# Fixed slots and a written TensorE order for the heads of a gated cross-attention block

## The chip, the core and the metric

The kernel runs on one core of a Trainium2 chip. The metric is the time of one execution in device microseconds (us). The engines are TensorE (PE; its weight loads are shown as PEld), VectorE (DVE), ScalarE (ACT), GpSimd (POOL) and SyncE (SP), which issues most DMAs.

## What is computed

The block has two gated halves over x of 8 batches x 256 tokens x 512 channels. First comes a cross-attention with 16 heads of 32 channels to a context of 256 rows per batch, in which the query and output projections are quantised to 8-bit integers. Then comes a feed-forward network (FFN) of 1408 hidden channels whose operands are quantised to fp8 after a reordering of columns.

```python
def xattn(x, cond, mask, wq, bq, wk, bk, wv, bv, wo, bo):   # 16 heads
    q = w8a8_linear(x, wq, bq); k = cond @ wk.T + bk; v = cond @ wv.T + bv
    ...
    scores = einsum('bhnd,bhld->bhnl', q, k) * inv_sqrt_d + mask[:, None]
    o = einsum('bhnl,bhld->bhnd', softmax(scores), v)
    return w8a8_linear(o, wo, bo)

def ffn(x, w_gate, w_up, w_down, up_idx, down_idx):
    qx, sx, sc = reorder_quantize_x(x, up_idx)               # fp8 grid
    t = silu(qlinear(qx, w_gate)) * qlinear(qx, w_up)
    return qlinear(reorder_quantize_x(t, down_idx), w_down)

x = x + tanh(g_xattn[0]) * xattn(layernorm(x), ctx, mask, ...)
x = x + tanh(g_ffn[0]) * ffn(layernorm(x), ...)
```

## The kernel before, in words

The program is one unrolled stream. A scheduler places the instructions of each engine by priority and by its own estimate of when operands are ready; that order is then fixed, and each engine executes its list in order, waiting on semaphores. `tc.keep_in_program_order` pins an instruction behind the one that was written before it on its engine. In the FFN all engines are pinned so (`InOrder`, seen as line L61). In the heads only the matmuls of one group of four heads, after the group's first, were pinned to each other (`in_turn`, with high priority).

**Start.** x, the context and the weights are loaded. The key and value weights are transposed in fp32; the query and output weights are quantised and transposed in bf16 (`prep_int8`, tiles `tb_wq`, `tb_wo`). Batch 0 gets its keys, queries and values.

**Heads.** The main loop runs over 8 batches x 8 slots (`NP` = 8, `B` = 8) and two more. Slot `g` is batch `b`, step `i`. The heads come in groups of four. Every second slot does the scores of a group (`scores`, L623, tile `s`): matmuls of 32 rows, four heads beside each other, into PSUM tiles of two banks (`ps_h`, two of them). DVE adds the mask, negates and finds the row's minimum (L638, `sn`, `nm`), ACT takes the exp (L648, `pr`). One slot later two heads are transposed (`transposed`, L664, tile `t`, copied to `pT` by ACT, L673), another slot later a group is multiplied with the values (`weighted`, L682, `poT`, copied to `oT`), and another slot later it is transposed back and normalised (`normalised`, L701 `po`, L705 `rsum`, L707 `o`).

Beside the heads each batch carries these steps:

- `project_kv` of the next batch: two context transposes (L501 `ct`, L504 `cT`), four key pieces (L511 `pk`, L518 `kT`), two value pieces (L527 `pv`, L534 `v`).
- `project_q` of the next batch: quantised rows (L552 `xq`, L560 `qx`), their transposes (L566 `qt`, L571 `qxT`) with a row broadcast of the scales (L356 `rb_sx`), then four query pieces (L577 `pq`, scaled on DVE L584, biased on POOL L587, `qT`).
- `project_out` of the batch before: rows (L225 `mxo`, L319, L320), transposes (L741 `ot`), two products (L752 `py`, L760 `y`), added to x on POOL (L763, L764).
- `quantise_x2` of the batch before: for each of two tiles, statistics and the fp8 grid (L775, L780 `xm`, L225 `mx`, L203, L207, L208), a transpose (`tb_x`), and a store to DRAM (L794).
- `pieces`: the FFN's weights, gathered by row through POOL's DMA queue (L425), masked on POOL (L431), quantised, transposed (`tb_gate`, `tb_up`, `tb_d`), stored and gathered again by column (L444, L477). There are 33 pieces over seven batches.

All of these except the scores use one pool of four PSUM banks (`bank`, tag `m`).

`spread` set the places: the steps of a list were appended to slots `first` to `end` at equal distances, with `kv_steps` from 0 to 6, `q_steps` from 3 to 7 (4 to 7 in batch 0), output and x2 from 3 to 8, pieces over the whole batch. In each slot the four head parts (lags 0 to 3) were written first and the slot's steps behind them:

```python
            for lag in range(4):
                if 0 <= g - lag < B * NP:
                    parts[(g - lag) // NP][lag]((g - lag) % NP)
            for f in slots[i]:
                f()
```

**FFN.** After the heads 16 token tiles pass through gate, up, silu, quantisation and down (L61). The last batch's output projection and x2 run beside its first tiles (`behind_heads`).

Of the kernel before, what the change touches and what calls it, by code (L numbers as in the profile page):

```python
# [29 lines left out]
F32 = mybir.dt.float32  # L30
# [20 lines left out]
class InOrder:  # L51


    def __init__(self, tc, engine):
        self.tc, self.engine = tc, engine

    def __getattr__(self, name):
        method = getattr(self.engine, name)

        def issue(*args, **kwargs):  # L60
            return self.tc.keep_in_program_order(method(*args, **kwargs))  # L61

        return issue
# [3 lines left out]
def tile_flamingo_block(  # L67
# [175 lines left out]
    with ExitStack() as actx:  # L243
# [4 lines left out]

        mv1 = wp.tile([P, NT, 2], F32, tag="mv1", name="mv1")
# [55 lines left out]
        def prep_fp32(n, rows):  # L305
            for k in range(KC):
                wr = rows[k]
                pt = bank(f"pt_{n}{k}")
                for cc in range(KC):
                    nc.tensor.transpose(  # L310
                        pt[:, cc * P : (cc + 1) * P], wr[:, cc * P : (cc + 1) * P], ident
                    )
# [9 lines left out]
        def transpose_bf16(src, dst, n, name):  # L322

            pt = bank(f"tb_{name}", BF16)
            for k in range(n):
                nc.tensor.transpose(
# [22 lines left out]
        def row_bcast(dst, cols, name):  # L349

            n = cols.shape[-1]
            for k0 in range(0, n, 4):
                m = min(4, n - k0)
                pb = bank(f"rb_{name}{k0}")
                for k in range(m):
                    nc.tensor.matmul(  # L356
# [9 lines left out]
        def held_up():  # L366
# [8 lines left out]
            for k in range(KC):  # L375
                oh = tl.tile([P, C], BF16, tag="q8", name=f"oh_{k}", bufs=4)
                nc.vector.tensor_scalar(oh, iota, u_f[:, k : k + 1], None, ALU.is_equal)
                nc.tensor.matmul(
# [13 lines left out]
        def held_down():  # L392
# [4 lines left out]
            for s0, n in ICH:  # L397
                pc = bank(f"count_d{s0}")
                nc.tensor.matmul(
# [93 lines left out]
        def project_kv(b, cr):  # L493
            cT = ld.tile([P, KC, L], F32, tag="cT", name=f"cT_{b}", bufs=1)
            kT = kv.tile([P, KC, L], F32, tag="kT", name=f"kT_{b}")
            v = []

            def transposed(lt):
                pt = bank(f"ct_{b}_{lt}")
                for cc in range(KC):  # L500
                    nc.tensor.transpose(  # L501
# [3 lines left out]
                    cT[:, :, lt * P : (lt + 1) * P], pt.rearrange("p (c o) -> p c o", o=P)  # L505
                )

            def keys(oc):
                pk = bank(f"pk_{b}_{oc}")
                for cc in range(KC):  # L510
                    nc.tensor.matmul(  # L511
                        pk[:, :L],
                        wTf["k"][:, cc, oc * P : (oc + 1) * P],
                        cT[:, cc, :],
# [7 lines left out]
            def values(lt):  # L522
# [3 lines left out]
                for cc in range(KC):  # L526
                    nc.tensor.matmul(  # L527
                        pv,
                        cT[:, cc, lt * P : (lt + 1) * P],
# [11 lines left out]
        def project_q(b):  # L541
            qT = kv.tile([P, KC, S], F32, tag="qT", name=f"qT_{b}")
            qxT = tl.tile([P, KC, S], BF16, tag="qxT", name=f"qxT_{b}")
            sxb = ld.tile([P, S], F32, tag="sxb", name=f"sxb_{b}", bufs=1)

            qx = {}
# [15 lines left out]
            def turned():  # L562
                pt = bank(f"qt_{b}", BF16)
                for nt in range(TPB):
                    for cc in range(KC):
                        nc.tensor.transpose(  # L566
# [3 lines left out]
                        )  # L570
                nc.any.tensor_copy(qxT, pt.rearrange("p (c n) -> p c n", n=S))  # L571
                row_bcast(sxb, sx[:, b * TPB : (b + 1) * TPB], f"sx{b}")

            def queries(oc):
                pq = bank(f"pq_{b}_{oc}")
                for cc in range(KC):
                    nc.tensor.matmul(  # L577
                        pq[:, :S],
                        wT8["q"][:, cc, oc * P : (oc + 1) * P],
                        qxT[:, cc, :],  # L580
# [4 lines left out]
                    qT[:, oc, :], pq[:, :S], s8["q"][:, oc : oc + 1], sxb, ALU.mult, ALU.mult  # L585
# [7 lines left out]
        def attention(b, qT, kT, v, mk):  # L593
# [9 lines left out]
            def in_turn(products):  # L603

                products[0]()
                with tc.high_priority():
                    for product in products[1:]:
                        tc.keep_in_program_order(product())

            def scores(i):  # L610
# [10 lines left out]
                def product(nt, h):  # L621
                    r0 = (h % HPC) * D
                    return nc.tensor.matmul(  # L623
# [7 lines left out]
                in_turn([partial(product, nt, h) for nt in range(TPB) for h in heads])  # L631
# [26 lines left out]
            def transposed(i):  # L658
                for h in (2 * i, 2 * i + 1):
                    pr = probs.pop(h)  # L660
                    pst = bank(f"t_{b}_{h}").rearrange("p (c n) -> p c n", n=S)
                    for nt in range(TPB):
                        for lc in range(LC):
                            nc.tensor.transpose(  # L664
# [11 lines left out]
            def weighted(oc):  # L676
# [3 lines left out]
                def product(lc, h):  # L680
                    r0 = (h % HPC) * D
                    return nc.tensor.matmul(  # L682
# [7 lines left out]
                in_turn([partial(product, lc, h) for lc in range(LC) for h in heads])  # L690
# [6 lines left out]
            def normalised(oc):  # L697
                oT = poT.pop(oc)
                po = bank(f"po_{b}_{oc}")
                for nt in range(TPB):  # L700
                    nc.tensor.transpose(  # L701
# [22 lines left out]
        def project_out(b, o):  # L724
            so = sm.tile([P, TPB], F32, tag="so", name=f"so_{b}")
            qoT = tl.tile([P, KC, S], BF16, tag="qxT", name=f"qoT_{b}")
# [10 lines left out]
            def turned():  # L737
                pt = bank(f"ot_{b}", BF16)
                for nt in range(TPB):
                    for cc in range(KC):  # L740
                        nc.tensor.transpose(  # L741
# [4 lines left out]
                nc.any.tensor_copy(qoT, pt.rearrange("p (c n) -> p c n", n=S))  # L746

            def product(nt):
                t = b * TPB + nt
                py = bank(f"py_{t}")  # L750
                for cc in range(KC):
                    nc.tensor.matmul(  # L752
                        py,
                        qoT[:, cc, nt * P : (nt + 1) * P],
# [13 lines left out]
        def quantise_x2(b):  # L768

            xT = tl.tile([P, KC, S], BF16, tag="x2T", name=f"x2T_{b}", bufs=1)  # L770

            def rows(nt):
                t = b * TPB + nt
# [115 lines left out]
        for g in range(B * NP + 2):  # L889
# [27 lines left out]
            for f in slots[i]:  # L917
                f()
# [212 lines left out]
```

## Time and profile before

| | us |
|---|---|
| median of 4 runs | 678.62 (674.23 to 678.92) |
| the profiled execution | 678.77 |
| its span, first to last instruction | 676.8 |
| mean granted TensorE clock | 0.887 |

Busy shares of the span on the page:

| PE | PEld | DVE | ACT | POOL |
|---|---|---|---|---|
| 525.4 us (78%) | 341.0 (50%) | 523.0 (77%) | 430.1 (64%) | 252.2 (37%) |

The shares are averages over stages with different limits, so a stage has to be read from its own windows. The matmuls are pipelined and their ends are modelled, so a PE that is busy is not a PE at its peak. The first scores start at 42.9 us, the scores of batches 1 to 7 at 102.1, 156.9, 212.0, 265.5, 319.3, 371.1 and 427.1 us, and the first matmul of the FFN at 495.1 us.

### The profile page before, as it was taken

What the parts mean: (1) busy time and instruction counts of PE and PEld (TensorE: products, weight loads), DVE (VectorE), ACT (ScalarE), POOL (GpSimd) and SP (SyncE); (2) the same over time, 40 slices, a digit from 0 to 9 for tenths busy, and PEclk for the clock granted to TensorE, in tenths of its full rate; (3) what the DMA queues carried; (4) which work ended last, traced back from release to release, by engine and by line L of the source; (5) the groups of instructions that cost most, each with busy time, mean ns of one, the idle gap of its engine ahead of it and who ended that gap; (6) DMA issues with size and microseconds to landing.
All of it is one profiled execution on the core that took longest, in us unless ns stands there. A gap on an engine that the chain in (4) does not pass through costs nothing.

```text
span 676.8 us, 10393 instructions
## 1 busy us (share of the span) xinstructions
PE 525.4 (78%) x3591; PEld 341.0 (50%) x3591; DVE 523.0 (77%) x1389; ACT 430.1 (64%) x995; POOL 252.2 (37%) x216
## 2 busy tenths in 40 slices
PE   2697786886994996996899696869387876999962
PEld 1465555654762663674575464447244543555531
DVE  1885696778759679779848899839759998899971
ACT  1467887737856874984894797555635666566661
POOL 4346054432441332433222004440034753477651
PEclk9798798895996997799599796979697998999996
DMA  8930013001250201300142213320000100011000
GB/s 219 356 80 11 24 48 94 17 15 47 64 171 26 85 1 32 94 17 16 32 170 77 74 56 94 109 78 1 7 11 23 50 22 31 32 40 41 31 32 31
DMA packets 27946, 41.64 MB, mean 62 GB/s; under 512 B 7563, under 2 KB 15115, under 8 KB 27894
## 3 DMA queue, kind: packets, MB, share of 16 engines
q1 hardware_dynamic: 19974, 28.25, 12.6%
q0 software_dynamic: 4336, 12.20, 6.2%
q10 hardware_dynamic: 3584, 0.54, 0.6%
q8 instruction: 28, 0.46, 0.3%
q14 instruction: 24, 0.20, 0.1%
HBM read 30.33 MB, written 10.65 MB: 61 GB/s over the span
## 4 chain that ended last, share of the span: by engine, by line
DVE 33%; PE 32%; ACT 17%; issue 9%; POOL 3%; DMA 2%; another core or an unknown queue 1%; ACTq 1%; POOLq 0%; DVEq 0%
PE pk L511 6%; PE t L664 6%; ACT pr L648 5%; DVE sn L638 3%; PE s L623 3%; PE poT L682 3%; DVE mxt L61 3%; PE pv L527 3%; ACT pT L673 3%; DVE s_gate L61 2%; PE p_gate L61 2%; DVE s_up L61 2%; PE p_up L61 2%; DVE xm L780 2%; ACT v_t L61 2%
## 5 line engine op out<-in xcount | busy, mean ns | idle before, releaser
L648 ACT ACTIVATE pr<-sn,nm 128x256 f32<-128x256 f32 x256 | 127.7, 503 | 46.9 <-DVE nm L638 46.7
L638 DVE CUSTOM_DVE_ANT_0 sn<-s,mk 128x256 f32<-128x256 f32 x256 | 97.9, 418 | 19.3 <-ACT pr L648 7.3
L664 PE MATMUL t<-ident,pr 128*128 128x128 f32 x512 | 81.3, 302 | 24.5 <-DVE v L534 12.0
L61 POOL TENSOR_TENSOR tt<-s_up,sl 128x704 f32<-128x704 f32 x32 | 64.9, 2029 | 81.1 <-ACT sl L61 58.4
L623 PE MATMUL s<-kT,qT 32*128 32x256 f32 x512 | 63.2, 492 | 33.1 <-DVE nm L638 23.5
L664 PEld LDWEIGHTS t<-ident,pr 128*128 128x128 f32 x512 | 63.7, 156 | 41.5 <-DVE v L534 13.6
L61 PEld LDWEIGHTS <-xg 128*128 128x128 bf16 x512 | 51.4, 101 | 54.0 <-issue 12.7
L673 ACT COPY pT<-t 128x512 f32<-128x512 f32 x120 | 65.6, 585 | 19.8 <-PE t L664 15.1
L511 PE MATMUL pk<-cT,wkT 128*128 128x256 f32 x256 | 69.4, 426 | 10.1 <-ACT cT L504 6.2
L511 PEld LDWEIGHTS pk<-cT,wkT 128*128 128x128 f32 x256 | 52.6, 213 | 25.1 <-ACT cT L504 6.4
L61 PE MATMUL p_gate<-gateT,xg 128*128 128x352 bf16 x256 | 46.1, 325 | 21.0 <-DVE s_gate L61 21.0
L623 PEld LDWEIGHTS s<-kT,qT 32*128 32x128 f32 x512 | 35.3, 223 | 49.4 <-issue 31.4
L763 POOL TENSOR_TENSOR x_sb<-x_sb,bo_b 128x512 f32<-128x512 f32 x16 | 22.6, 1426 | 96.9 <-ACT xq L552 96.9
L527 PE MATMUL pv<-wvT,cT 128*128 128x512 f32 x128 | 58.3, 599 | 0.1
L648 ACT ACTIVATION_READ_ACCUMULATOR pr<-sn,nm 128x1 f32 x256 | 49.3, 193 | 0.0
L587 POOL TENSOR_SCALAR qT<-qT,bq_c 128x256 f32<-128x256 f32 x32 | 17.9, 567 | 83.6 <-DVE qT L584 62.1
L61 PE MATMUL p_up<-upT,xg 128*128 128x352 bf16 x256 | 46.5, 328 | 0.0
L61 PE MATMUL yp<-wdT,qtT 128*128 128x512 bf16 x176 | 42.4, 391 | 1.9 <-ACT qtT L61 1.9
L61 ACT COPY qtT<-ptq 128x1024 bf16<-128x1024 bf16 (+1 forms) x32 | 22.3, 748 | 32.0 <-PE ptq L61 32.0
L61 ACT ACTIVATE v_t<-tt,rs_t 128x1408 f32<-128x1408 f32 x16 | 23.5, 1470 | 27.9 <-DVE rs_t L61 27.9
L682 PE MATMUL poT<-pT,v 128*32 128x256 f32 x512 | 39.2, 430 | 1.1 <-ACT cT L504 0.7
L527 PEld LDWEIGHTS pv<-wvT,cT 128*128 128x128 f32 x128 | 23.3, 191 | 26.6 <-issue 24.6
(192 smaller groups left out, 1105.7 us busy)
## 6 DMA issues: line engine op xcount, KB each, us to landing
cr<-in_ctx_dram SPq DMA_DIRECT2D x8, 512.0 KB
x_sb<-in_x_dram SPq DMA_DIRECT2D x8, 512.0 KB
out_dram<-yo SPq DMA_DIRECT2D x16, 256.0 KB
wd<-in_L_ffn_w_down_dram SPq DMA_DIRECT2D x4, 704.0 KB
mk<-in_mask_BxSxS_ff_dram SPq DMA_DIRECT2D x8, 256.0 KB
scr_x<-x2T SPq DMA_DIRECT2D x8, 256.0 KB
scr_gate<-gateT SPq DMA_DIRECT2D x1, 1408.0 KB
scr_up<-upT SPq DMA_DIRECT2D x1, 1408.0 KB
```

The lines of the kernel that those rows point to most:

```text
L61: return self.tc.keep_in_program_order(method(*args, **kwargs))
L511: nc.tensor.matmul(pk[:, :L], wTf["k"][:, cc, oc * P : (oc + 1) * P], cT[:, cc, :], start=(cc == 0), stop=(cc == KC - 1),)
L527: nc.tensor.matmul(pv, cT[:, cc, lt * P : (lt + 1) * P], wTf["v"][:, cc, :], start=(cc == 0), stop=(cc == KC - 1),)
L587: nc.gpsimd.tensor_scalar(qT[:, oc, :], qT[:, oc, :], bq_c[:, oc : oc + 1], ISD, ALU.add, ALU.mult)
L623: return nc.tensor.matmul(pss[h][:, nt, :], qT[r0 : r0 + D, oc, nt * P : (nt + 1) * P], kT[r0 : r0 + D, oc, :], start=True, stop=True,)
L638: nc.vector.tensor_tensor_reduce(out=sn[:, nt, :], in0=pss[h][:, nt, :], in1=mk[:, nt, :], scale=-1.0, scalar=3.0e38, op0=ALU.add, op1=ALU ...
L648: nc.scalar.activation(pr[:, nt, :], sn[:, nt, :], AF.Exp, bias=nm[:, nt : nt + 1], scale=-1.0, accum_out=sums[:, nt, h : h + 1],)
L664: nc.tensor.transpose(pst[:, lc, nt * P : (nt + 1) * P], pr[:, nt, lc * P : (lc + 1) * P], ident,)
L673: nc.scalar.copy(pT, pst)
L682: return nc.tensor.matmul(poT[oc][r0 : r0 + D, :], v[0][:, lc, h * D : (h + 1) * D], probsT[h][:, lc, :], start=(lc == 0), stop=(lc == LC ...
L763: nc.gpsimd.tensor_tensor(x_sb[:, t, :], x_sb[:, t, :], bo_b, ALU.add)
L780: nc.vector.scalar_tensor_tensor(xm, x_sb[:, t, :], mv[:, 0:1], mu_b, ALU.subtract, ALU.mult)
```

## The change

Four things are edited together.

1. `in_turn` goes, and all TensorE instructions of the attention stage are issued through `ten`, an `InOrder` whose `kept` is switched on at the first slot. From there TensorE follows the written order. The other engines are still placed by the scheduler.
2. `spread` goes. An `agenda` over all 66 slots takes the steps at slot numbers counted from the batch's start, which may reach into the next batch: the last two key pieces, the second value piece and the last three query pieces of the next batch now stand in that batch's own slots 0 to 3, and the last step of x2 one slot later than the batch's end.
3. Within a slot the steps are no longer all behind the four head parts: a third of them stands behind each of the first three (scores, transposes, products); a single step stands behind the third.
4. Some tiles (`cT`, `qxT`, `sxb`, `qoT`, `x2T`) are allocated at their first use and not when the steps are listed.

```diff
-    def __init__(self, tc, engine):
-        self.tc, self.engine = tc, engine
+    def __init__(self, tc, engine, kept=True):
+        self.tc, self.engine, self.kept = tc, engine, kept
...
-            return self.tc.keep_in_program_order(method(*args, **kwargs))
+            i = method(*args, **kwargs)
+            return self.tc.keep_in_program_order(i) if self.kept else i
...
+        ten = InOrder(tc, nc.tensor, kept=False)
...
-            def in_turn(products):
-
-                products[0]()
-                with tc.high_priority():
-                    for product in products[1:]:
-                        tc.keep_in_program_order(product())
...
-                in_turn([partial(product, nt, h) for nt in range(TPB) for h in heads])
+                for nt in range(TPB):
+                    for h in heads:
+                        product(nt, h)
...
-        def spread(slots, steps, first, end):
-
-            for k, f in enumerate(steps):
-                slots[first + k * (end - first) // len(steps)].append(f)
+        agenda = [[] for _ in range(B * NP + 2)]
+
+        def due(b, steps, slots):
+
+            for f, i in zip(steps, slots, strict=True):
+                agenda[b * NP + i].append(f)
+
+        def evenly(n, first, end):
+            return [first + k * (end - first) // n for k in range(n)]
+
+        KV_AT = (4, 4, 5, 6, 8, 10, 7, 9)
+        Q_AT = (4, 5, 7, 8, 10, 11)
+
+        OUT_AT = (3, 4, 4, 5, 6, 7, 8, 8)
+        PIECES_AT = (0, 1, 2, 4, 5)
...
-                    spread(slots, kv_steps, 0, 6)
-                    spread(slots, q_steps, 4 if b == 0 else 3, 7)
+                    due(b, kv_steps, KV_AT)
+                    due(b, q_steps, Q_AT)
...
-                    spread(slots, project_out(b - 1, o_last) + quantise_x2(b - 1), 3, NP)
+                    due(b, project_out(b - 1, o_last) + quantise_x2(b - 1), OUT_AT)
...
-                    spread(slots, pieces[n0:n1], 4 if b == 0 else 0, NP)
+                    due(b, pieces[n0:n1], evenly(n1 - n0, 4, NP) if b == 0 else PIECES_AT[: n1 - n0])
...
+            ten.kept = True
+
+            n = len(agenda[g])
             for lag in range(4):
                 if 0 <= g - lag < B * NP:
                     parts[(g - lag) // NP][lag]((g - lag) % NP)
-            for f in slots[i]:
-                f()
+                for f in agenda[g][n * lag // 3 : n * (lag + 1) // 3]:
+                    f()
```

## Prediction

> **What bounds the kernel now.** I read the busy time by stage first, cut where the first scores matmul (L623) of each batch starts. The columns are the length, then the busy time of PE, PE's weight loads, DVE, ACT and POOL (instructions in brackets), the granted TensorE clock and the DMA load.
>
> ```profile
> core 0: us, PE busy (x) PEld busy (x) DVE busy (x) ACT busy (x) POOL busy (x), PEclk, DMA share, GB/s
> 51.70:102.10 50.40, 40.26 (x269) 27.49 (x268) 35.92 (x117) 41.19 (x102) 20.27 (x21) 0.90 0.10 28
> 102.10:156.90 54.80, 41.55 (x294) 28.39 (x294) 41.02 (x124) 33.43 (x92) 21.46 (x19) 0.92 0.13 39
> 156.90:212.00 55.10, 46.00 (x325) 30.43 (x325) 39.97 (x135) 37.42 (x105) 18.75 (x18) 0.84 0.27 87
> 212.00:265.50 53.50, 44.53 (x322) 29.58 (x322) 42.38 (x137) 38.83 (x108) 16.95 (x16) 0.88 0.13 40
> 265.50:319.30 53.80, 46.47 (x328) 30.90 (x329) 45.47 (x144) 39.70 (x110) 19.26 (x18) 0.85 0.15 45
> 319.30:371.10 51.80, 47.45 (x323) 31.36 (x323) 37.78 (x132) 39.92 (x115) 11.03 (x12) 0.84 0.27 91
> 371.10:427.10 56.00, 42.86 (x303) 28.40 (x302) 51.02 (x149) 42.66 (x113) 9.93 (x10) 0.85 0.22 68
> 427.10:495.10 68.00, 45.80 (x389) 31.79 (x388) 46.92 (x153) 37.78 (x109) 16.40 (x18) 0.82 0.17 51
> 495.10:676.80 181.70, 139.62 (x894) 80.48 (x890) 150.47 (x194) 98.07 (x106) 96.35 (x58) 0.93 0.09 31
> ```
>
> A batch takes about 54 us (the rows are batches 0 to 7 and the FFN), and no engine is full: in batches 1 to 6 PE is busy for 76 to 92%, DVE for 73 to 91%, ACT for 61 to 77%. The next view cuts batch 4 and its neighbours where the character of the work changes.
>
> ```profile
> 258.00:280.80 22.80, 15.61 (x103) 9.43 (x100) 19.62 (x75) 16.37 (x47) 6.13 (x7) 0.63 0.14 40
> 280.80:312.00 31.20, 31.20 (x237) 21.81 (x239) 26.05 (x70) 23.39 (x62) 13.13 (x12) 1.00 0.15 48
> 312.00:335.40 23.40, 16.05 (x102) 9.77 (x94) 20.20 (x74) 17.07 (x48) 4.32 (x5) 0.64 0.08 23
> ```
>
> So a batch is two stages. For 31 us PE is never idle, at full clock. For 23 us DVE is 86% busy (19.62 of 22.80), PE has little to do, and its clock falls to 0.63. The work is not too much; it is bunched. The order of TensorE's instructions shows why: all projections of the next batch stand between its scores 1 and 3, and after scores 3 come only scores, transposes and the quantising of x2. The waits from 257 to 281 us agree:
>
> ```profile
> ACT v_x L203 <- DVE rs_x L214: 5.2, 1, 5.2
> ACT pr L648 <- DVE nm L638: 3.9, 1, 3.9
> PE s L623 <- DVE mx L212: 3.2, 1, 3.2
> PE t L664 <- DVE v L534: 1.4, 1, 1.4
> ```
>
> The chain of waits for the same stretch alternates between the quantising of x2 and the softmax:
>
> ```profile
> 262.34 0.89 DVE xm L780
> 263.25 0.69 DVE mx L225
> 264.32 4.04 ACT pr L648 x16
> ```
>
> **The change, part by part.** *No arithmetic is added or removed.* Matmuls, copies and DMAs are the same; only their places move. In the built programs the FFN's TensorE order is the same in both, so its 181.7 us stays.
>
> *The start.* With TensorE's order pinned, the first scores stand behind the values and all four transposes of wo. Before, they started at 42.9 us, but scores 1 only at 51.7 us, with one wo transpose left. I start the heads at 52.0 us, and the first group's softmax, which lay beside the values, now comes after: 2.8 us of DVE (eight at 0.344), so 3 us.
>
> *Even slots.* In the built program each pair of slots (four heads) now has TensorE work of about the same kind. From full-clock paces, the distance from one start to the next in an unbroken run (a keys piece 8 x 0.216 = 1.73 us, a values piece 8 x 0.429 = 3.43, two heads' transposes 1.04, 16 scores matmuls 1.08, 16 of poT 1.0, half of py 0.9, pq 0.5, small transposes and row broadcasts 0.3 to 0.6) the four pairs of a steady batch sum to about 11.3, 7.8, 11.6 and 10.7 us: 41 us. Before, the 31.2 us dense stretch plus about 8 us of full-clock work in the sparse one (its instructions at the same paces) give the same 39. DVE's pairs, from its paces (a head's softmax 2 x 0.344, x2 rows 3.6 a tile, a weight piece about 2.2) are 9.3, 10.2, 14.3 and 8, or 42. ACT has about 39. So no engine needs over 42 to 46 us of the 54.
>
> *The limit after.* The most loaded engine becomes DVE. How full can it be? Where it led, it was 86% busy (258 and 312 us, above); in the dense stretch 83% (26.05 of 31.20). I take 0.85 for all, with 0.80 and 0.92 as ends. Batches 1 to 6 hold 41.02+39.97+42.38+45.47+37.78+51.02 = 257.6 us of DVE. At 0.85 that is 303 us against 325 (102.1 to 427.1); at 0.92, 280; at 0.80, 322.
>
> *Batch 0.* Half of the next batch's projections leaves it for batch 1, and ACT is its fullest engine (41.19). Less two kT copies, 40 at about 0.89: 45 us, and the 3 of the start make 48, against 50.4.
>
> *Batch 7.* It took 68 us, with PE and DVE under 70%. It now receives the rest of its own projections (two pk, one pv, three pq). Its pairs sum to PE 15, 8, 6, and DVE about 10 each, so 35 us to its last scores. From there quantising x2 ended the stage: py at 472.2, its transpose at 488.2, the first p_gate at 495.1, 23 us. The second py now stands before the last scores, so I take 18.
>
> *POOL's and SP's queues.* The gather of w_down (L477) now has all eleven issues ahead of qT of batch 7; before, seven were ahead of the second. The store landed about 6.3 us after issue (428.3 to 434.6) and the gathers took 14.8 (434.6 to 449.4). That is 21 us from the middle of pair 3 of batch 6, and batch 7's scores come 18 later: 3 us of stall, with 0 and 10 as ends, all of TensorE behind it. Similarly qT of scores 1 stands behind one or two weight gathers (L425, whose landing POOL waited for by up to 4.4 us); its slack is a slot of 6 us, so I price it at 0, at most 2 us a batch. SP's stores of x2T move by one slot; each is needed batches later. The gather of x (L190) goes behind the w_down gathers, with 50 us left: nothing.
>
> *PSUM banks.* TensorE now waits in written order for four shared banks. After the scores, the copies pT of heads 3 and 4 stand behind eight exps on ACT: 1.1 (scores) + 0.5 (first sn) + 4.0 (eight exps: the 4.04 us row, whose x16 counts each with its accumulator read) + 0.4 (kT) + 1.0 = 7.0 us. TensorE has 4.8 us of work ahead that needs no freed bank, and DVE frees two more. I count 0.6 us a pair, inside the 0.85; its upper end, 2.2 us a pair, is a rival below.
>
> *The clock.* In all stretches where PE was dense the granted clock was 1.00; where it was under 70% busy it was 0.63 to 0.64. Idle stretches that I expect after are 1 to 3 us, so I take full clock and 41 us. [...] Were the clock to stay at a mean of 0.85, PE's 41 would become about 47 a batch, still under the 303/6 = 50.5 that I forecast, and the sum would move by perhaps 10 us.
>
> *Sum:* 52 + 48 + 303 + (35 + 3 + 18) + 181.7 = 640.7 us of span. The profiled execution took 678.77 us with a span of 676.8, so 2.0 lie outside; its time is 0.15 above the median of 678.62. That makes 642.7, and I say **643 us**. With 0.92 and no POOL stall it is 617; with 0.80 and 10 us of stall, 669.
>
> **The rivals.** *Partial gain (663 to 675):* DVE's third pair (14.3 us) stands in its queue ahead of the next softmax, so exps start late and the 2.2 us of bank wait comes up in about half of the 32 pairs: 16 x 1.6 more = 26, so 669. For it: DVE's load is uneven over the pairs. Against it: DVE pieces have slack and may slide into the fourth pair.
>
> *Slower (about 705):* the strict order takes back more than evenness gives. The place is a TensorE instruction that waits for a DVE or ACT result while ready work stands behind it: transposes for exps, the first scores for qT (queries of slot 7 are needed in slot 8, through DVE and POOL), banks for pT. The heads now have 443.4 us (51.7 to 495.1) for 33 pairs, 13.4 us each. With 41/4 = 10.3 us of TensorE work the break-even is a stall of 3.1 us a pair; at 4 us it is 14.3 x 33 + 52 + 181.7 + 2, or about 708. For it: exps behind a late DVE would give just such stalls, and the waits on DVE above are of 1.4 to 3.9 us. Against it: the hardware runs either order as built, so today's order pays such waits too (PE t for DVE v: 7 times, 12.0 us), and lags of a slot lie between producer and user.
>
> *No change (675 to 682):* the period is set by a loop of softmax, copy and bank that no placing alters. Against it: the dense stretch turned 11 heads (45 transposes) in 31 us without PE idling, 2.8 us a head against 3.4 over the whole batch.
>
> **How the numbers follow.** No change means within 0.5%, 3.4 us, about what a measurement of this kernel can tell. Forecast (617 to 663): 0.60. Partial gain: 0.14. No change: 0.06. Slower: 0.17. Faster than 617, DVE over 0.92: 0.03. Faster by over 0.5% is 0.60 + 0.14 + 0.03 = 0.77. The range from 617 to 682 holds 0.60 + 0.14 + 0.06 = 0.80.
>
> **What would show it.** Right: scores of neighbouring groups start 11 to 14 us apart instead of 6 to 26; batches of 47 to 53 us with DVE near 85%; PEclk near 1.0 from 60 us to the FFN; FFN near 182 us. Wrong: PE waiting for pT, exps or qT for over 3 us in each pair; a clock of 0.5 in the heads; DVE under 78%; a longer FFN.

## The result, and the profile after

The change makes the kernel slower: 709.94 us median of 22 runs (704.93 to 717.58) against 676.0 us for the kernel before (32 runs, measured beside them). The ratio is 1.0504, with a 95% interval of 1.0481 to 1.0528. The profiled execution took 713.98 us with a span of 712.1. The forecast was 643; the rival "slower (about 705)" came true.

The busy time by stage, cut at the first scores of each batch as before (after the change all of TensorE's instructions in the heads show line L61, that of the helper which pins them, so they are told by their tiles):

```profile
core 0: us, PE busy (x) PEld busy (x) DVE busy (x) ACT busy (x) POOL busy (x), PEclk, DMA share, GB/s
52.30:109.30 57.00, 35.49 (x246) 23.15 (x244) 39.69 (x131) 44.71 (x117) 25.09 (x23) 0.76 0.14 38
109.30:165.80 56.50, 44.04 (x324) 29.52 (x324) 41.10 (x142) 37.91 (x106) 17.24 (x16) 0.91 0.11 33
165.80:225.80 60.00, 45.06 (x320) 29.85 (x320) 40.76 (x133) 36.35 (x103) 18.21 (x18) 0.89 0.25 80
225.80:288.30 62.50, 48.27 (x326) 31.43 (x324) 43.39 (x143) 41.50 (x113) 18.45 (x17) 0.84 0.13 39
288.30:347.20 58.90, 43.83 (x332) 29.88 (x332) 40.19 (x138) 37.52 (x106) 16.16 (x15) 0.91 0.11 32
347.20:404.50 57.30, 44.46 (x319) 28.56 (x319) 41.02 (x130) 36.21 (x104) 11.11 (x12) 0.91 0.28 95
404.50:476.80 72.30, 50.78 (x358) 33.54 (x356) 51.03 (x154) 47.15 (x124) 17.51 (x19) 0.83 0.20 64
476.80:531.70 54.90, 42.72 (x342) 29.11 (x342) 39.17 (x131) 29.34 (x88) 7.84 (x9) 0.88 0.09 25
531.70:712.10 180.40, 139.19 (x894) 79.95 (x890) 149.22 (x194) 98.08 (x106) 96.97 (x58) 0.92 0.10 33
```

Against the rows of before: the start is 0.6 us later, batch 0 is 6.6 longer, batches 1 to 6 are 42.5 longer (367.5 against 325.0), batch 7 is 13.1 shorter and the FFN 1.3 shorter. That sums to the 35.3 us by which the span grew. No engine works more. Over the whole span PE is busy for 523.8 us (before 525.4), DVE for 518.0 (523.0) and ACT for 425.5 (430.1). Of the 42.5 us by which batches 1 to 6 grew, 7.5 are busy time of PE, while batches 0 and 7 lost 7.9 of it. The other 35.0 are time in which PE stands idle: 367.5 less 276.4 busy is 91.1 us, or 3.8 in each of the 24 pairs of slots; before it was 325.0 less 268.9, which is 56.1, or 2.3.

The chain that ended last, by engine and by line, shows where that idle time is spent. First the kernel before, then the change:

```profile
DVE 33%; PE 32%; ACT 17%; issue 9%; POOL 3%; DMA 2%; another core or an unknown queue 1%; ACTq 1%; POOLq 0%; DVEq 0%
PE pk L511 6%; PE t L664 6%; ACT pr L648 5%; DVE sn L638 3%; PE s L623 3%; PE poT L682 3%; DVE mxt L61 3%; PE pv L527 3%; ACT pT L673 3%; DVE s_gate L61 2%; PE p_gate L61 2%; DVE s_up L61 2%; PE p_up L61 2%; DVE xm L780 2%; ACT v_t L61 2%
```
```profile
PE 30%; DVE 25%; ACT 24%; issue 11%; POOL 3%; DMA 3%; another core or an unknown queue 1%; ACTq 1%; POOLq 0%; DVEq 0%
ACT pr L649 13%; PE pv L61 7%; PE t L61 4%; PE pk L61 4%; PE poT L61 3%; DVE mxt L61 3%; PE py L61 3%; DVE s_gate L61 2%; DVE sn L639 2%; DVE s_up L61 2%; PE p_gate L61 2%; PE s L61 2%; PE p_up L61 2%; ACT v_t L61 1%; ACT pT L674 1%
```

The exps (`pr`) went from 5% of the path to 13% of a longer one: from about 35 us to about 90 (5.2% of 676.8 us, 12.7% of 712.1). Yet no large wait of TensorE names them. What PE waited for from 109.3 to 476.8 us (batches 1 to 6; total, times, longest):

```profile
PE ot L61 <- ACT cT L510: 24.4, 5, 6.3
PE pv L61 <- ACT pT L674: 17.0, 5, 5.2
PE tb_x L61 <- ACT kT L524: 8.1, 3, 4.3
```

These are no waits for an operand. `ot` does not read `cT`, nor `tb_x` `kT`: they wait for the PSUM bank that the copy `cT` or `kT` frees. All the waits of this kind that end with a copy on ACT sum to 58.3 us of the 91. Before, in its batches 1 to 6 (102.1 to 427.1 us), they summed to 6.8. Its largest waits were others, the first of them for the two-bank tile of the scores, which the softmax on DVE frees:

```profile
PE s L623 <- DVE nm L638: 23.5, 15, 4.0
PE s L623 <- DVE mx L212: 9.6, 3, 3.2
PE t L664 <- DVE v L534: 8.6, 5, 2.6
```

The timeline of batch 4 after the change shows what the copies themselves stand behind (start, length, engine, what; in brackets the idle time before it):

```profile
288.32 1.15 PE L61 MATMUL s<-kT,qT 32*128 32x256 f32 x16 [0.56 <-POOL qT L593]
289.39 1.99 PE L61 MATMUL pk<-cT,wkT 128*128 128x256 f32 x8
290.79 0.69 DVE L226 TENSOR_REDUCE mx_up<-wr_up 128x1 f32<-128x512 f32 x1 [1.40 <-POOL wr_up L435]
291.81 0.42 DVE L639 CUSTOM_DVE_ANT_0 sn<-s,mk 128x256 f32<-128x256 f32 x1
292.58 0.49 ACT L649 ACTIVATE pr<-sn,nm 128x256 f32<-128x256 f32 x1
296.51 0.45 ACT L524 ACTIVATE kT<-pk,bk_c 128x256 f32<-128x256 f32 x1
297.02 0.38 PE L61 MATMUL tb_x<-ident_b,q 128*128 128x128 bf16 x4 [4.32 <-ACT kT L524]
```
```profile
317.13 1.15 PE L61 MATMUL s<-kT,qT 32*128 32x256 f32 x16
318.21 1.09 PE L61 MATMUL ct<-ident,cr 128*128 128x128 f32 x8
319.14 1.04 PE L61 MATMUL t<-ident,pr 128*128 128x128 f32 x8
319.52 0.51 ACT L649 ACTIVATE pr<-sn,nm 128x256 f32<-128x256 f32 x1
323.47 1.05 ACT L510 COPY cT<-ct 128x512 f32<-128x512 f32 x2
324.09 0.61 PE L61 MATMUL ot<-ident_b,qo 128*128 128x128 bf16 x8 [3.91 <-ACT cT L510]
```

In the first, `pk` is done at 291.4, but its copy starts at 296.51, when the eighth exp is over. In the second, two `ct` and two `t` fill all four shared banks 3 us after the scores began, and the first of their copies stands behind eight exps too. In written order TensorE does nothing else meanwhile: it stands idle for 4.32 us before `tb_x` and for 3.91 us before `ot`. The four banks are used in turn, but in these two stretches that does not cover the time for which the copies stand in ACT's queue behind the exps (292.58 to 296.51 us in the first, 319.52 to 323.47 in the second).

### The profile page after: what moved, and what is told of

Read it like the earlier page. It is cut to its first block, busy times and chain, and to the rows that moved or that the text cites. A ratio compares the mean times of both kernels' runs of the same rounds, so it can differ in the third digit from the quotient of the medians.

```text
span 712.1 us, 10403 instructions
## 1 busy us (share of the span) xinstructions
PE 523.8 (74%) x3591; PEld 336.4 (47%) x3591; DVE 518.0 (73%) x1393; ACT 425.5 (60%) x990; POOL 250.3 (35%) x216
## 4 chain that ended last, share of the span: by engine, by line
PE 30%; DVE 25%; ACT 24%; issue 11%; POOL 3%; DMA 3%; another core or an unknown queue 1%; ACTq 1%; POOLq 0%; DVEq 0%
ACT pr L649 13%; PE pv L61 7%; PE t L61 4%; PE pk L61 4%; PE poT L61 3%; DVE mxt L61 3%; PE py L61 3%; DVE s_gate L61 2%; DVE sn L639 2%; DVE s_up L61 2%; PE p_gate L61 2%; PE s L61 2%; PE p_up L61 2%; ACT v_t L61 1%; ACT pT L674 1%
## 5 line engine op out<-in xcount | busy, mean ns | idle before, releaser
L639 DVE CUSTOM_DVE_ANT_0 sn<-s,mk 128x256 f32<-128x256 f32 x256 | 95.3, 418 | 17.9 <-PE s L61 7.1
L61 POOL TENSOR_TENSOR tt<-s_up,sl 128x704 f32<-128x704 f32 x32 | 65.5, 2046 | 78.6 <-ACT sl L61 56.4
L61 PE MATMUL t<-ident,pr 128*128 128x128 f32 x512 | 78.7, 303 | 17.0 <-ACT pr L649 14.2
L61 PE MATMUL pv<-wvT,cT 128*128 128x512 f32 x128 | 74.4, 736 | 22.8 <-ACT pT L674 17.0
L61 PEld LDWEIGHTS t<-ident,pr 128*128 128x128 f32 x512 | 64.6, 154 | 32.8 <-ACT pr L649 17.4
L61 PEld LDWEIGHTS <-xg 128*128 128x128 bf16 x512 | 50.5, 100 | 51.9 <-issue 12.3
L61 PE MATMUL pk<-cT,wkT 128*128 128x256 f32 x256 | 68.8, 419 | 6.2 <-ACT cT L510 6.2
L593 POOL TENSOR_SCALAR qT<-qT,bq_c 128x256 f32<-128x256 f32 x32 | 16.0, 501 | 147.4 <-DVE qT L590 112.4
L61 PEld LDWEIGHTS pk<-cT,wkT 128*128 128x128 f32 x256 | 52.3, 215 | 18.1 <-ACT cT L510 6.4
L61 PE MATMUL p_gate<-gateT,xg 128*128 128x352 bf16 x256 | 44.8, 319 | 20.8 <-DVE s_gate L61 20.8
L61 PEld LDWEIGHTS pv<-wvT,cT 128*128 128x128 f32 x128 | 29.6, 243 | 58.3 <-issue 38.4
L61 PE MATMUL yp<-wdT,qtT 128*128 128x512 bf16 x176 | 44.9, 408 | 1.9 <-ACT qtT L61 1.9
L61 PE MATMUL p_up<-upT,xg 128*128 128x352 bf16 x256 | 44.8, 319 | 0.0
L697 ACT COPY oT<-poT 128x256 f32<-128x256 f32 x32 | 11.9, 372 | 49.7 <-PE poT L61 47.1
L61 PE MATMUL s<-kT,qT 32*128 32x256 f32 x512 | 38.6, 417 | 3.8 <-POOL qT L593 3.6
L61 PE MATMUL poT<-pT,v 128*32 128x256 f32 x512 | 37.6, 415 | 4.1 <-ACT pT L674 4.1
L61 ACT COPY qtT<-ptq 128x1024 bf16<-128x1024 bf16 (+1 forms) x32 | 22.3, 748 | 30.5 <-PE ptq L61 30.5
L61 ACT ACTIVATE v_t<-tt,rs_t 128x1408 f32<-128x1408 f32 x16 | 23.5, 1470 | 27.0 <-DVE rs_t L61 27.0
L540 DVE TENSOR_TENSOR v<-pv,bv_b 128x512 f32<-128x512 f32 x16 | 11.0, 690 | 38.1 <-PE pv L61 35.3
```

Of the source, the lines that this page charges most:

```text
L61: i = method(*args, **kwargs)
L540: nc.vector.tensor_tensor(v[0][:, lt, :], pv, bv_b, ALU.add)
L593: nc.gpsimd.tensor_scalar(qT[:, oc, :], qT[:, oc, :], bq_c[:, oc : oc + 1], ISD, ALU.add, ALU.mult)
L639: nc.vector.tensor_tensor_reduce(out=sn[:, nt, :], in0=pss[h][:, nt, :], in1=mk[:, nt, :], scale=-1.0, scalar=3.0e38, op0=ALU.add, op1=ALU ...
L697: nc.scalar.copy(oT, poT[oc])
```

## The experiments

My theory after this: written order makes TensorE wait for banks whose copies stand behind the burst of eight exps in ACT's queue. The rivals: the new slots themselves are the loss; the softmax is late in DVE's queue; data is late everywhere and the bank is only the last wait to be seen. All ratios are to the kernel before, measured beside each run.

### Order or slots: e1, e2, e3

e1 keeps the new slots and the dealing in thirds, and gives TensorE's order back to the scheduler:

```diff
-                for nt in range(TPB):
-                    for h in heads:
-                        product(nt, h)
+                in_turn([partial(product, nt, h) for nt in range(TPB) for h in heads])
...
-            ten.kept = True
```

> The new slots and the dealing in thirds, but TensorE's instructions are not held in written order (scores and weighted products are kept together as in the kernel before). Theory 'order' (TensorE in written order waits for PSUM banks whose copies stand behind exps on ACT, 4 us a pair of slots): the stalls go, 650 to 680 us. Theory 'slots' (the new places of the steps, weight pieces and x2 ahead of the softmax in DVE's queue, are themselves the loss): still 695 to 715 us.

e2 is the other half: `spread` and its slots, with the pinned order.

```diff
-                    due(b, kv_steps, KV_AT)
+                    spread(slots, kv_steps, 0, 6)
...
             ten.kept = True
```

> The slots of the kernel before and all steps behind the parts, but TensorE held in written order from the first slot of the heads. Theory 'order': slower than before by as much as the change, 695 to 715 us. Theory 'slots': within 1% of before, 670 to 685 us. If the two only hurt together, both this and the run with free order lie near 680.

e3 keeps slots and order, and writes all steps of a slot behind its parts:

```diff
-                for f in agenda[g][n * lag // 3 : n * (lag + 1) // 3]:
-                    f()
+            for f in agenda[g]:
+                f()
```

> The change with its slots and its pinned order, but all steps of a slot written behind the four parts instead of in thirds between them. If the dealing was what put keys and values in front of transposes that are late: 690 to 700 us. If the dealing is neutral: 706 to 714. If it helped (fills waits for the softmax): 720 to 735.

Measured: e1 678.27 us, ratio 1.0003 [0.9949, 1.0058]; e2 735.5, 1.0846 [1.0786, 1.0907]; e3 712.42, 1.0515 [1.0456, 1.0574]. So the new slots in the scheduler's order change nothing, the old slots in written order cost 8.5%, and within the written order the new slots give 3.4 points of it back. The dealing does not change the time. Theory "order" holds, though e2 lies above its 695 to 715 us, and "slots" falls. With the old slots TensorE waited from 112.7 to 425.5 us mostly for DVE, and these waits are of up to 8.2 us:

```profile
PE tb_x L61 <- DVE q L209: 24.0, 6, 8.2
PE tb_x L61 <- DVE o L710: 20.4, 4, 5.2
PE ct L61 <- DVE o L710: 20.2, 4, 8.2
```

e3 takes as long as the change, but TensorE waits for other things in it (109.0 to 472.0 us):

```profile
PE s L61 <- POOL qT L593: 16.3, 8, 3.9
PE t L61 <- ACT pT L674: 12.2, 7, 3.3
PE ct L61 <- DVE o L710: 10.8, 5, 2.6
```

Its waits for banks behind copies on ACT sum to 20.5 us, not 58.3. Another 32.0 are for banks that DVE frees with `o`, which stands among the `sn` of the softmax in DVE's queue (as at 304.2 and 305.2 us). So copies on ACT are not the only way in which a written order loses this time.

### Mending single waits: e4, e6, e7

e4 writes a slot's transposes ahead of its scores, so that their copies come before the exps; e6 also puts `py` a slot behind its transposes; e7 leaves the order and moves the copies cT and kT from ACT to DVE.

```diff
-            for lag in range(4):
+            for third, lag in enumerate((1, 0, 2, 3)):
```
```diff
-        OUT_AT = (3, 4, 4, 5, 6, 7, 8, 8)
+        OUT_AT = (3, 4, 5, 6, 7, 8, 9, 9)
```
```diff
-                nc.scalar.copy(
+                nc.vector.tensor_copy(
                     turned[0][:, :, lt * P : (lt + 1) * P], ...
...
-                nc.scalar.activation(
-                    kT[:, oc, :], pk[:, :L], AF.Identity, bias=bk_c[:, oc : oc + 1]
+                nc.vector.tensor_scalar(
+                    kT[:, oc, :], pk[:, :L], bk_c[:, oc : oc + 1], None, ALU.add
```

> The change with one thing altered: in a slot the transposes of the probabilities of the slot before are written ahead of the slot's scores, so their copies to SBUF stand ahead of the eight exps on ACT and their banks come free early. Theory 'order, banks behind exps': 16 waits of 2 to 4 us go, 660 to 690 us. Theory 'softmax late in DVE's queue': the same stall moves to the scores, 700 to 720 us.

> Transposes ahead of scores as in e4, and OUT_AT = (3, 4, 5, 6, 7, 8, 9, 9): py one slot behind the transposes that it multiplies, not in the same slot, and x2 one slot later. In e4 TensorE waited in batches 1 to 5 for 24.1 us for qoT (py L61 <- DVE qoT). Theory 'written order without a slot of distance between producer and user': those waits go and nothing as large takes their place, 670 to 688 us. Rival 'the softmax in DVE's queue sets the pace': the wait moves to another product, 695 to 708 us.

> The change with the copies cT and kT (which free the banks of ct and pk) on DVE, and so out from behind the exps in ACT's queue; everything else as in the change. Theory 'banks behind exps': the waits ot <- cT (24.4 us in batches 1 to 5), tb_x <- kT (8.1) and po <- kT (2.9) go, 670 to 692 us. Rival 'DVE's queue is as late as ACT's': they turn into waits for DVE, 703 to 725 us.

Measured: e4 701.93 us, ratio 1.0356 [1.0285, 1.0428]; e6 712.24, 1.0503 [1.0436, 1.057]; e7 698.12, 1.0291 [1.023, 1.0352]. e4 and e7 gain 8 and 12 us of the 34 lost, less than the theory asked, and e6 loses e4's gain again. e4's time lies in the range of the rival "softmax late in DVE's queue" (700 to 720), though the stall did not move to the scores. PE's largest waits between 110 and 400 us show why, in e4 and then in e6:

```profile
PE py L61 <- DVE qoT L749: 24.1, 5, 5.3
PE t L61 <- ACT pr L649: 14.5, 13, 2.8
```
```profile
PE t L61 <- ACT pr L649: 28.7, 16, 5.2
PE t L61 <- DVE qT L590: 8.9, 4, 2.4
```

In e4 the wait of `ot` for cT is no longer among the large ones, and TensorE stands before `py` instead; with `py` moved in e6, it stands before the transposes, for the exps. In these two runs a wait taken out of the fixed order is replaced by the next late item; that this goes on as long as the exps come late is my reading.

### Fewer and more banks: e9, e10, e14, e15

e9 is the change and e10 is e1, each with three shared banks in place of four. e14 and e15 (the change, and e1) write the transposes of the slots without scores to the two-bank tiles that the scores leave idle there.

```diff
-    ps_m = ctx.enter_context(tc.tile_pool(name="ps_m", bufs=4, space=PSUM))
+    ps_m = ctx.enter_context(tc.tile_pool(name="ps_m", bufs=3, space=PSUM))
```
```diff
-                    pst = bank(f"t_{b}_{h}").rearrange("p (c n) -> p c n", n=S)
+                    pst = bank(f"t_{b}_{h}") if i % 2 else two_banks(f"t_{b}_{h}")[:, 0, :]
+                    pst = pst.rearrange("p (c n) -> p c n", n=S)
```

> The change with three shared PSUM banks in place of four. Theory 'banks': in written order each missing bank costs much, 735 to 780 us. If the waits are for data and not for banks: 710 to 722 us.

> The new slots in free order (as e1), with three shared PSUM banks in place of four. Theory 'order and banks together': a free order passes the late bank, 678 to 695 us, that is less than half of what the pinned order loses. If banks cost the same in either order: as much slower than 678 as the pinned one is slower than 710.

> The change, with the transposes of two heads in the slots without scores written to the two-bank tiles that the scores leave idle there: eight of the 47 bank uses of a batch leave the shared banks, TensorE's order is unchanged. Theory 'banks behind exps': 25 us or more below the change measured beside it. Theory 'data late, banks only seen last': within 8 us of it. Rival 'the next scores wait for the copies': above it.

> The new slots in free order with the same eight transposes in the idle two-bank tiles. If banks also hold the free order: 10 to 25 us below the kernel before. If not, within 6 us of it.

Measured: e9 752.94 us, ratio 1.1088 [1.1025, 1.115], 43 us above the change; e10 702.63, 1.0356 [1.0292, 1.0419], 24 above e1. Banks are scarce in either order, in the written one 1.8 times as much; my "less than half" was missed. e14 took 713.3 us (1.0514 [1.0485, 1.0544]) beside the change at 716.64, so 3 us less: the theory's 25 failed, and the rival "data late, banks only seen last" had asked for just this (within 8 us). The trace of e14 offers another reason, that I freed the wrong banks: the jam of `ct`, `ct`, `t`, `t` is in the slots with scores, and the wait stayed:

```profile
PE ot L61 <- ACT cT L510: 22.4, 4, 6.2
```

e15 took 700.24 us (1.0311 [1.0288, 1.0334]), 22 more than e1, though it only has more banks. The scheduler built another order from it, with scores 15.9, 8.1, 18.9 and 14.9 us apart in batch 2, where e1 has 8.2, 14.7, 6.1 and 25.7 and the change 16.3, 9.0, 19.4 and 15.2. So a free order is not good in itself; what it happens to interleave seems to decide.

### The exps and their burst: after_again, e17, e18, e19

These change the exps themselves. after_again is the change itself, as the measure on the chip of e14, e15 and e17. e17 (the change) and e18 (e1) have one exp a head in place of two; they use the first row tile's maximum for both and leave out the second one's sum, so they compute something else:

```diff
-                        nc.scalar.activation(
-                            pr[:, nt, :],
-                            sn[:, nt, :],
...
+                    nc.scalar.activation(
+                        pr,
+                        sn,
+                        AF.Exp,
+                        bias=nm[:, 0:1],
+                        scale=-1.0,
+                        accum_out=sums[:, 0, h : h + 1],
+                    )
...
-                nc.vector.reciprocal(rsum[:, :, hs], sums[:, :, hs])
+                nc.vector.reciprocal(rsum[:, 0, hs], sums[:, 0, hs])
```

> The change itself once more, beside the other runs of this call on the same chip. Any theory: 1.05 of before, 705 to 716 us where before takes 675 to 680; on a chip where before takes 664, either 697 (the same ratio) or still 708.

> The change, with one exp instruction a head over 512 columns in place of two over 256 (it uses the maximum of the first row tile for both and leaves out the second row tile's sum, so it computes something else): ACT's work of four heads falls from 4.0 to about 2.5 us. Theory 'TensorE waits for copies behind the exps': 1.5 us in about 20 pairs, so 25 to 40 us less than the change. If the exps are not on the path: under 10 us.

> The new slots in free order (as e1), with the single exp instruction a head of e17 (the second row tile's maximum and sum are left out, so it computes something else). Theory 'only the written order has the exps on its path': under 15 us below the kernel before, against the 43 us that e17 took off the pinned order. If the exps set the pace in either order: 30 to 45 us below the kernel before.

Measured: after_again 716.64 us, ratio 1.0555 [1.0533, 1.0577]; e17 674.0, 0.9925 [0.9905, 0.9945]; e18 661.08, 0.9738 [0.9689, 0.9788]. The ratio of after_again is 0.5 points above the first one, more than either interval allows, so half a point between two sets of runs tells nothing here. The groups of the exps, first in after_again and then in e17 (busy us, mean ns of one):

```profile
L649 ACT ACTIVATE pr<-sn,nm 128x256 f32<-128x256 f32 x256 | 126.5, 495 | 42.2 <-DVE nm L639 41.8
```
```profile
L649 ACT ACTIVATE pr<-sn,nm 128x512 f32<-128x512 f32 x128 | 91.7, 718 | 59.4 <-DVE nm L639 58.8
```

ACT has 34.8 us less of exps, and the pinned kernel is 42.6 us faster, so the exps lay on its path. Part of the gain went with the clock: it was granted at 0.918 in e17 and at 0.892 in after_again, and in batches 1 to 6 PE was busy for 263.3 us in e17 (97.5 to 429.3 us), for 276.4 in the change. In the free order the same cut is worth about 18 us (2.65% from e1's ratio): a little over the 15 I had set, and under half of what the pinned order gains. With one exp a head the written order is 1.9 points behind the free one; with two it is 5.0 to 5.5 behind.

e19 changes no work and no instruction of TensorE's order (both traces show the same sequence of matmuls in the heads and the FFN). It writes the softmax of heads 2 and 3 of a group one slot later, so that at most four exps stand together in program order:

```diff
             def scores(i):
                 if i % PPC:
+                    late.pop()()
                     return
...
-                for h in heads:
-                    sn = at.tile(...)
+                def softmax(some):
+                    for h in some:
+                        sn = at.tile(...)
...
+                softmax(heads[:2])
+                late.append(partial(softmax, heads[2:]))
```

> The change with the softmax of a group of four heads written in two halves, heads 0 and 1 in the slot of the scores and heads 2 and 3 in the next; TensorE's order is unchanged. The copies that free banks then stand behind four exps (2 us) at most in ACT's queue, not eight (4 us). Theory 'copies behind the burst of exps': 2 us in 16 to 20 pairs, 670 to 690 us where the kernel before takes 678. If only the total of ACT's work on the path counts: 700 to 716 us. If the scores' tiles, held longer, stop the next scores: above 716.

Measured: 682.05 us, ratio 1.0062 [1.0014, 1.0111]. Of the 5.0% that the change loses, 4.4 points come back. The same places of batch 4 as above:

```profile
273.05 1.99 PE L61 MATMUL pk<-cT,wkT 128*128 128x256 f32 x8
276.88 0.49 ACT L653 ACTIVATE pr<-sn,nm 128x256 f32<-128x256 f32 x1
278.85 0.45 ACT L524 ACTIVATE kT<-pk,bk_c 128x256 f32<-128x256 f32 x1
279.35 0.38 PE L61 MATMUL tb_x<-ident_b,q 128*128 128x128 bf16 x4 [3.00 <-ACT kT L524]
```
```profile
PE ot L61 <- ACT cT L510: 8.1, 3, 2.9
```

kT now comes 2.0 us after the first exp, not 3.9, and the wait for cT falls from 24.4 us to 8.1. In batches 1 to 6 (107.9 to 445.5 us) PE's idle time falls from 91.1 us to 66.6, and all its waits for banks behind copies on ACT fall from 58.3 to 36.9. In the kernel before, copies lie between exps without anyone having asked for it:

```profile
274.30 0.59 ACT L673 COPY pT<-t 128x512 f32<-128x512 f32 x1 [0.75 <-PE t L664]
274.78 0.51 ACT L648 ACTIVATE pr<-sn,nm 128x256 f32<-128x256 f32 x1
275.29 0.50 ACT L648 ACTIVATE pr<-sn,nm 128x256 f32<-128x256 f32 x1
276.09 0.59 ACT L673 COPY pT<-t 128x512 f32<-128x512 f32 x1 [0.22 <-PE t L664]
```

I counted in the traces how often all eight exps of a group run on ACT with nothing between them: 12 of 32 groups before, 10 in e1, 18 in the change, 24 in e2, 22 in e3, 19 in e9 and in e15, 17 in e14, 15 in e6, 14 in e7, 11 in e10, 10 in e4, 1 in e19. Roughly these numbers rise with the times, but not as a rule: e4, with 10, takes 702 us, and e15, with one more than the change, is faster than it. e19 halves the burst on DVE as well as on ACT, so the two are not separated by it alone. e17, which shortens ACT's part and leaves DVE its eight `sn`, speaks for ACT.

### On another chip: e8, e11, e12, e13

These four ran on a chip on which the kernel before took 663.76 us, 2% less than on the others, for a reason I did not find; no run of the change was made there. So only their traces and large differences count. e8 has other slots for the pieces, e11 is e4 and e7 together, e12 (the change) and e13 (e1) put `ct` and `pv` into the idle two-bank tiles.

```diff
-        PIECES_AT = (0, 1, 2, 4, 5)
+        PIECES_AT = (1, 1, 3, 5, 7)
```
```diff
-                pt = bank(f"ct_{b}_{lt}")
+                if lt == 0:
+                    turned.append(two_banks(f"ct_{b}"))
+                pt = turned[1][:, lt, :]
...
-                pv = bank(f"pv_{b}_{lt}")
+                pv = two_banks(f"pv_{b}_{lt}")[:, 0, :]
```

> The change with PIECES_AT = (1, 1, 3, 5, 7): the weight pieces in the slots without scores, so that they no longer stand in DVE's queue ahead of a softmax waiting for POOL's mask. Rival 'softmax late behind the pieces in DVE's queue': the first exp of a pair comes up to 2 us sooner, 685 to 700 us. Theory 'banks behind exps': the exps still hold the copies, 703 to 716 us.

> Transposes ahead of scores (as e4) and the copies cT and kT on DVE (as e7) together. If both take away parts of one cause, banks that wait behind exps, their gains of 8 and 12 us add: 683 to 693 us. If each only moves the stall to the next late item, 695 to 705 us.

> The change with ct and pv in the two-bank tiles of the scores, which are idle after the softmax: no instruction moves, but four of the 47 bank uses of a batch leave the four shared banks. Theory 'banks': ot no longer waits for cT (24.4 us in five batches) nor pv for pT (17.0 in six), 665 to 690 us. Theory 'data late, banks only the last to be seen': 700 to 712 us. Rival 'the scores now wait for them': above 712.

> The new slots in free order (as e1), with ct and pv in the two-bank tiles of the scores. If banks limit the free order too (it lost 24 us with three banks): 655 to 672 us, better than the kernel before. If it already passes the late bank by other work: 673 to 685 us.

Measured: e8 726.01 us (ratio 1.0921 [1.0879, 1.0962]), e11 707.57 (1.0661 [1.0602, 1.072]), e12 709.06 (1.0675 [1.0624, 1.0726]), e13 674.07 (1.016 [1.012, 1.0199]). e8 speaks against the rival "softmax late behind the pieces", which asked for 685 to 700: its largest wait is again for cT, with 35.1 us; it also lies above the 703 to 716 of the theory. e11 did not add the gains of its parts. e12 moved the wait for cT to the front: `ct` waited for the softmax that frees its two-bank tile, 16.3 us, and for cT, 12.4. Its time, like that of e14, lies where "data late, banks only the last to be seen" had put it. I read all three as the same stall in another place, which is not shown; how much of each is the chip stays open. e13 is 1.6% slower than the kernel before, where e1 was as fast: as in e15, more banks did not help the free order.

## Why the prediction was wrong, and where it was right

**Right.** The heads start at 52.3 us (52.0 predicted). Batch 7 takes 54.9 (56): 37.2 to its last scores (38) and 17.7 from there to the first `p_gate` (18). The FFN takes 180.4 (181.7). The stall for POOL's gathers at batch 7 is 1.4 us, within 0 and 10. DVE's work in batches 1 to 6 is 257.5 us, and 257.6 was counted.

**The clock.** I took full clock; the rows show 0.83 to 0.91 in batches 1 to 6, where before they showed 0.84 to 0.92. PE was busy for 46.1 us a batch there, not 41. That is near what I gave for a mean clock of 0.85, where I also divided wrongly: 41 us at 0.85 make 48, not 47. That idle stretches of 1 to 3 us leave the clock full was my estimate. The idle stretches after the change were of up to 6.3 us, and a stretch of before speaks against the estimate too: behind an idle time of 3.2 us the granted clock is 0.50 from 157.0 to 171.6 us, although PE is busy for 12.00 of these 14.60 us and idle for at most 1.4 at a time. In batches 1 to 6 the new places cost no clock: its mean is 0.88 there, and before it was 0.86. In batch 0 the clock fell from 0.90 to 0.76, with PE busy for 62% of it and not 80%; no run tells why.

**Batch 0.** 57.0 us, not 48. I counted 40 us of ACT at a share of 0.89; it was 44.7 at 0.78. No row had shown 0.89 (before, ACT was busy for 41.19 of 50.40 us, 0.82), and the first group's exps, which ran ahead of this window before, were counted for DVE alone. `t` waited twice for exps, 9.1 us together. Batch 0 is 9 of the 71 us by which the span was missed (712.1 against 640.7).

**The failed step** is "I count 0.6 us a pair, inside the 0.85". The sum let DVE's busy share set the length of batches 1 to 6 and had no term for TensorE's waits. DVE is 70% busy there (257.5 of 367.5), which makes 367.5 us where the sum had 303: 64.5 of the 71 us. I took 0.85 from stretches in which DVE set the pace, but after the change it does not. The length is PE's 276.4 us of work and 91.1 of idle time. Of the idle time 58.3 us, or 2.4 a pair, are waits for banks behind copies on ACT: four times my 0.6, and a little over the 2.2 that I had given as the upper end. The rest of the 3.8 a pair had no term.

The working had the right mechanism, exps ahead of the copies in ACT's queue. Its 7.0 us from the scores to the copy came out in the pair at 317 us (324.09 less 317.13), but by luck in the terms: the first exp started 2.4 us after the scores, not 1.6, and TensorE went on after one copy cT, not after a kT and two pT. "4.8 us of work ahead that needs no freed bank" was 3.1 there (317.13 to 320.18), since two `ct` and two `t` took all four banks. In the pair at 288 us the copy kT ended after 8.6 us, since DVE's first `sn` came 3.5 us after the scores began, behind a weight piece that waited for POOL. So the stall is 3.9 and 4.3 us in these two pairs.

**What is shown and what is not.** That the written order costs the time is shown by e1, and that most of it goes through the burst of the softmax, ACT's exps above all, by e17 and e19. That the path from the exps to TensorE is the banks is read from the traces. e3 and e6 lose as much with fewer waits for copies on ACT, and e12 and e14 freed banks with little gain or none, so how much of the loss goes by the banks stays open.

**The rivals.** "Slower" was priced at a stall of 4 us a pair, 14.3 us for each of 33 pairs and 708 in all. Measured are 14.5 us for each of 33 pairs (52.3 to 531.7). In batches 1 to 6 a pair has 3.8 us of idle time and 11.5 of work, where the rival had 4 and 10.3. I argued against it that a slot lies between producer and user. That is true of operands, and the long waits were not for operands but for banks, which are freed by a copy that belongs to another step. I also argued that the built order before pays such waits too. It does (2.3 us a pair), but less, and only 6.8 us in all are for banks behind copies on ACT. Whether that is because copies lie between the exps in its ACT queue, or because its TensorE order is another, no run separates. The chance of 0.17 for this rival was too low. The evenness, from which all of the gain was to come, was not reached: scores were to start 11 to 14 us apart, and in batch 2 they are 16.3, 9.0, 19.4 and 15.2 apart. So no run tells what it would be worth.

## What to carry to other kernels

When TensorE's order is fixed, count for each shared PSUM bank what stands ahead of its copy in the queue of the engine that copies, not only when the operands are ready; in the two pairs shown, TensorE stood idle for the time by which this was longer than its work in free banks (4.3 and 3.9 us). Break long bursts on the copying engine (here eight exps, 4 us) into pieces with the copies between them: splitting one softmax in two, with all of TensorE's order unchanged, gave back 4.4 of 5.0 points. An engine's share of busy time from a stretch that it led (here 0.85) did not carry over to one where it waits (0.70).

## What the runs showed of the hardware

An exp of 128x256 with its row sum took 0.495 us and one of 128x512 took 0.718, so 256 more columns cost 0.22 us; that the rest, 0.27 us, is paid once for each instruction is an estimate from these two means (after_again and e17). Halving the number of exps was worth 2.65% even in the free order (e18 against e1). One chip ran the kernel before 2% faster than the others (663.76 us against 676 to 679), which is as much as many of the differences here and stays unexplained. Of the kernels that do the whole computation none beat the kernel before; e1 with its softmax in halves would be the next to try, and was not run.
